# Adding the down projection's results on GpSimd in the next stage, and spreading VectorE's small work

## The chip, the cores and the metric

One core of a Trainium2 chip runs the whole kernel. The metric is the device time of one execution in microseconds, and lower is better. Profile figures come from one profiled execution.

## The reference

2048 rows (tokens) of 1024 columns pass through three residual blocks: a gated feed-forward with 4-bit weights, a state-space convolution along the 1024 columns, and the same feed-forward again.

```python
def _dequant(qweight, scales, qzeros, g_idx):
    # W[k,n] = scales[g_idx[k],n] * (w4[k,n] - (z4[g_idx[k],n]+1)), groups of 128 rows
def _L0_ffn_ref(x, ...):                     # 1024 -> 2752 -> 1024
    h = jax.nn.silu(xf @ Wg) * (xf @ Wu)
    out = h @ Wd
def _L0_attn_ref(u, ...):                    # one S4 response K for all rows
    y = irfft(rfft(u, n=2*L) * rfft(K, n=2*L), n=2*L)[..., :L]
    return y + D[0] * u
x = L0_attn_u                                # (2, 1024, 1024)
x = x + 0.5 * _L0_ffn_ref(_layernorm(x), ...)
x = x + _L0_attn_ref(_layernorm(x), ...)
x = x + 0.5 * _L0_ffn_ref(_layernorm(x), ...)   # the same weights
```

## The kernel before, in words

**Jobs.** The rows are cut into four blocks `b` of 512 rows, each of four tiles of 128 rows. A block goes through the feed-forward twice (k = 1 and k = 3), so there are eight jobs (b, k) in the order (0,1), (1,1), (0,3), (1,3), (2,1), (3,1), (2,3), (3,3). Each job has two stages. *Up* (`gate_up`) has 64 steps: eight waves of weight columns times eight groups of 128 input rows. A wave has three pairs of gate and up columns (six units of 128 columns; waves 5 and 6 have two pairs, the last two and a half). *Down* (`down`) has 44 steps: two halves `a` of 512 output columns times 22 tiles of the inner 2752.

**Scaling in the bank.** Each group of 128 input rows has its own scale, so after a group's products a PSUM bank is multiplied by the ratio of this group's scale to the next one's, and the next group's products are added to it. This is `scaled`: on ScalarE (L729) for units with an even number, else on VectorE (L733); some odd units go to ScalarE too, in jobs and steps listed in `gate_up`. TensorE multiplies each weight tile by two parts of the input, `xTh` (float32r) and `xTl` (float16), L764; in down by `hh` and `hl`, L840. At a wave's end ScalarE takes silu (L792), VectorE multiplies gate and up (L795), and GpSimd splits the result in two (L797, L799).

**Weights.** They are kept in DRAM as signed bytes. SP loads the bytes of a step four steps ahead (`b`, `bd`; L690, L697), and GpSimd casts them three steps ahead (L706; in job 0 ScalarE casts some). Job 0 also makes those bytes from the packed words on the way (`raw`, L580 to L584 on VectorE).

**Results of down.** They come out transposed. ScalarE and VectorE write them, scaled, into `yT[a]`; VectorE transposes it in blocks of 32 (`turn_block`, L875); SP writes it to DRAM (`rows_out`, `yz`) and reads it back by rows (`rows_in`, `yr`); VectorE adds it to x in pieces of 256 columns (`back`, L893). Half 0 of a job goes through this in the second half of the same down, half 1 in the first steps of the next job's up. Only the last half of the last job goes through TensorE instead: 16 transposes into PSUM (`back_by_products`, L899) and four adds of 512 columns (L901).

**Normalization.** `moments_by_tile` takes two statistics a tile of rows (L189) and joins them (L192); `guess` starts an inverse square root from the bits (L199 to L203), and `deviations` refines it by three of Newton's steps of three small operations each (L214 to L216) and one last multiply (L217), all on 128 x 4 elements. After k = 1, the next job's up also holds the convolution of the block that has just come out of its first feed-forward: norm (L225), transposes, products (L1197), adds (L1227 to L1237), then moments and `deviations` again for k = 3. `normalize` (L258) is the norm of the next job's input. Job 1's up also makes the response tables (`s4_tables`, between L927 and L1170) in pieces.

**Order.** `hooks` hold work by step: `at(up, s, f)` calls f at step s of up, `at(dn, d, f)` at step d of down; half steps lie in the middle of a step's products. `in_order_of_writing(f, engine)` keeps the instructions of f behind what was written before for that engine. What is not pinned so is placed by a list scheduler with its own estimates, and TensorE, VectorE, ScalarE, GpSimd and SP each run their list strictly in order.

Of the kernel before, what the change touches and what calls it, by code (L numbers as in the profile page):

```python
# [18 lines left out]
ALU = mybir.AluOpType  # L19
# [38 lines left out]
def macaron_s4_kernel(  # L58
# [149 lines left out]
    def deviations(b, k, factor=1.0):  # L208


        mv, ve, r = ln.pop(b)
        e = small.tile([P, NT], F32, tag="e", name=f"e_{b}_{k}")
        for three in (3.0, 12.0, 768.0):
            nc.vector.tensor_tensor(e, r, r, ALU.mult)  # L214
            nc.vector.tensor_tensor(e, e, ve, ALU.mult)
            nc.vector.scalar_tensor_tensor(r, e, three, r, ALU.subtract, ALU.mult)  # L216
        nc.vector.tensor_scalar(r, r, -factor / 8192, None, ALU.mult)  # L217
        for t in range(NT):
            ln[b, t] = (mv[:, t, 0:1], r[:, t : t + 1], k)
        return r  # L220
# [198 lines left out]
    def scales_down():  # L419
        ps = bank("ps_d")  # L420
        for i in range(2):
            row, turn = t2(f"drow_{i}"), t2(f"dturn_{i}")
            nc.sync.dma_start(row[:GD], down_s[:, bass.ts(i, 512)])
            nc.vector.tensor_copy(by_chunk(turn[:GD]), by_block(row[:GD]))
            for k in range(4):
                nc.tensor.transpose(
                    ps[:, bass.ts(4 * i + k, GD)], turn[:GD, bass.ts(k, P)], ident[:GD, :GD]
                )
        n = NC * GD
        flat = s_dn.rearrange("p c g -> p (c g)")  # L430
        nc.vector.tensor_copy(flat, ps[:, :n])
        inv = t2("inv_d")[:, :n]
        inverse(inv, flat, "d")
        inv = inv.rearrange("p (c g) -> p c g", c=NC)
        nc.vector.tensor_tensor(
            ratd[:, :, : GD - 1], s_dn[:, :, : GD - 1], inv[:, :, 1:], ALU.mult
        )
        nc.vector.tensor_scalar(
            ratd[:, :, GD - 1 :], s_dn[:, :, GD - 1 :], 0.5 / EIGHT, None, ALU.mult
        )  # L440
# [294 lines left out]
    def gate_up(j, b, hooks):  # L735
        hi, lo = pieces[b]
        ps = {}
        for s, (wi, g) in enumerate(STEPS):
# [13 lines left out]
            for i, (k, pos, done) in enumerate(turns):  # L752
# [21 lines left out]
                if g < GK - 1:  # L774
                    on_act = unit % 2 == 0
                    if pos == 1:
                        on_act = (j == 0 and g % 4 == 0) or (j == 1 and s < 32 and g % 2 == 0)
                        on_act = on_act or (j in (2, 5, 6) and 10 <= s < 20 and g % 2 == 0)
# [84 lines left out]
    by_products = lambda j, a: j == len(JOBS) - 1 and a == NH - 1  # L863
# [24 lines left out]
    def back(b, a, i):  # L888

        t, half = divmod(i, 2)  # L890
# [573 lines left out]
    def rows_home(at, hooks, b, a, turned_at, out_at, in_at, added_at):  # L1464

        pinned = lambda f, *e: lambda: in_order_of_writing(f, *e)
        for i in range(8):
            at(hooks, turned_at[i], pinned(lambda i=i: turn_block(a, i), ET.DVE))
            at(hooks, added_at[i], pinned(lambda i=i: back(b, a, i), ET.DVE))
        for i in range(4):  # L1470
            at(hooks, out_at[i], pinned(lambda i=i: rows_out(a, i), ET.SP))
            at(hooks, in_at[i], pinned(lambda i=i: rows_in(b, a, i), ET.SP))

    def fast():
# [5 lines left out]
        for j, (b, k) in enumerate(JOBS):  # L1480
# [7 lines left out]
            pinned = lambda f, *e: lambda: in_order_of_writing(f, *e)  # L1488
            if prev:
                pb, pk = prev  # L1490
                turned_at = [i / 2 for i in range(8)]
                added_at = [10 + (i if j == 1 else i / 2) for i in range(8)]
                rows_home(at, up, pb, 1, turned_at, (5, 5, 6, 6), (8, 8, 9, 9), added_at)
                if pk == 1:
                    late = 34 if j == 1 else 14
                    first = 30 if j == 1 else 14
                    steps = [(up, first + (5 * i // 4 if j == 1 else (3 * i // 2) / 2)) for i in range(8)]
                    in_pieces(at, steps, lambda: moments_by_tile(pb, 2, halves=True))
                    at(up, late + 7, pinned(lambda: deviations(pb, 2), ET.DVE))
# [19 lines left out]
                    at(up, late + 27, lambda: moments(pb, 3))  # L1519
                    at(up, late + 28, lambda: deviations(pb, 3, LIFT))  # L1520
# [5 lines left out]
                    at(up, late + 28, save)  # L1526
# [9 lines left out]
            if j == 0:  # L1536
# [6 lines left out]
                at(up, 40, scales_down)  # L1543
# [13 lines left out]
            if after:  # L1557
                ab, ak = after
                if ak == 1:
                    at(up, 55 if j == 0 else 6, lambda: load_x(ab, rows_of(u, ab)))  # L1560
                    if j == 0:
                        steps = [(dn, d) for d in range(4, 22, 2)]
                        in_pieces(at, steps, lambda: moments_by_tile(ab, 1, halves=True))
                        newton = lambda: deviations(ab, 1, LIFT)
                        at(dn, 21, lambda: in_order_of_writing(newton, ET.DVE))
                    else:
                        steps = [(up, s) for s in range(18, 27)]
                        in_pieces(at, steps, lambda: moments_by_tile(ab, 1, halves=True))
                        newton = lambda: deviations(ab, 1, LIFT)
                        at(up, 28, lambda: in_order_of_writing(newton, ET.DVE))  # L1570
# [9 lines left out]
                for t in range(NT):  # L1580
                    for half in range(2):
                        d, where = ((22 + 4 * t + 2 * half, dn), (3 * t + half, dn))[min(j, 1)]
                        if j > 1:
                            d, where = (45 if ak == 3 else 31) + 2 * t + half, up
# [3 lines left out]
                    if j == 0:  # L1588
                        for half in range(2):
                            piece = lambda t=t, half=half: turn_by_pool(ab, t, half)  # L1590
                            at(dn, 24 + 4 * t + 2 * half, piece)
# [10 lines left out]
            turned_at = [22.5 + i if j == 0 else 22 + i / 2 for i in range(8)]  # L1602
            added_at = [37.5 + (3 * i // 2) / 2 if j == 0 else 34.5 + i for i in range(8)]
            out_at, in_at = (((31, 31, 32, 32), (35, 35, 36, 36)), ((27, 27, 28, 28), (31, 31, 32, 32)))[min(j, 1)]
            rows_home(at, dn, b, 0, turned_at, out_at, in_at, added_at)
            for t in range(NT) if not after else ():
                at(dn, int(added_at[2 * t + 1]) + 2, lambda t=t: store_half(t, 0, nc.sync))
# [207 lines left out]
```

## Time and profile before

| what | us |
|---|---|
| runs, median of 3 | 2099.97 (2099.79 to 2103.26) |
| the profiled execution | 2098.86 |
| its span, first to last instruction | 2097.1 |
| TensorE busy | 2044.3 |
| VectorE busy | 1722.2 |
| ScalarE busy | 1405.3 |
| GpSimd busy | 1301.5 |

The profiled execution is 1.76 us longer than its span: that lies before the first and after the last instruction. A matmul's record covers its passage through the array and overlaps the next one's, so busy shares of TensorE are no measure of its rate. In the rows, a line such as L733 is the line of the kernel's source, `out<-in` are tiles without numbers, and after the bar stand the busy time of the group in us, the mean of one in ns, and the idle time of its engine just before, with what ended it.

### The profile page before, as it was taken

To read this page: it belongs to the slowest core of one execution; us is meant where nothing else is said; L and a number is where in the kernel's file an instruction comes from. 1 tells how busy PE (TensorE), PEld (TensorE's weight loads), DVE (VectorE), ACT (ScalarE), POOL (GpSimd) and SP (SyncE) were. 2 spreads that over 40 slices of the span, in tenths; PEclk is the share of its full clock that TensorE was granted. 3 is DMA by queue.
4 is the path that set the end of the run, shared out by engine and by line. 5 is a ranking of instruction groups with operands and counts; after the bars stand their busy time and mean duration, and the time that the engine had idled before them with its cause. 6 is when DMAs were issued, how large, how long until landed. Compare 5 with 4: busy or idle time off the path is not lost.

```text
span 2097.1 us, 30092 instructions
## 1 busy us (share of the span) xinstructions
PE 2044.3 (97%) x9316; PEld 1378.3 (66%) x9316; DVE 1722.2 (82%) x2916; ACT 1405.3 (67%) x2200; POOL 1301.5 (62%) x1688
## 2 busy tenths in 40 slices
PE   6999999999999999999999999999999999999998
PEld 4555675577767667655766567676686676866576
DVE  8888978778889878897788878888788878787777
ACT  6777787646675577677767776755777647767775
POOL 5867758646855468555866568544685546865542
PEclk9999999999999999999999999999999999999999
DMA  4324342112621126511462126211163111651113
GB/s 146 117 85 146 111 125 74 34 53 55 167 78 44 42 51 167 158 34 35 113 169 96 31 51 165 81 38 49 38 161 98 40 47 34 161 166 51 35 34 100
DMA packets 280039, 182.47 MB, mean 87 GB/s; under 512 B 100667, under 2 KB 259236, under 8 KB 279870
## 3 DMA queue, kind: packets, MB, share of 16 engines
q1 hardware_dynamic: 278566, 178.06, 30.8%
q8 instruction: 76, 1.25, 0.2%
q10 hardware_dynamic: 1016, 1.82, 0.2%
q14 instruction: 93, 0.76, 0.1%
q0 software_dynamic: 288, 0.59, 0.1%
HBM read 120.18 MB, written 41.23 MB: 77 GB/s over the span
## 4 chain that ended last, share of the span: by engine, by line
PE 86%; DVE 7%; DMA 2%; POOL 2%; issue 1%; ACT 1%; SPq 0%; ACTq 0%; POOLq 0%; DVEq 0%
PE pg L764 52%; PE po L840 28%; PE pc L1197 3%; DVE pg L733 2%; PE pb L1197 1%; DMA bd<-wdq 1%; DVE po L733 1%; PE st L232 1%; DVE x L893 1%; DMA b<-wq 1%; POOL q L613 0%; POOL hl L799 0%; DVE x L258 0%; DVE ve L199 0%; DMA x<-in_L_attn_u_dram 0%
## 5 line engine op out<-in xcount | busy, mean ns | idle before, releaser
L729 ACT ACTIVATE pg<-pg,rat 128x512 f32<-128x512 f32 x1255 | 794.5, 661 | 388.0 <-PE pg L764 387.0
L733 DVE TENSOR_TENSOR pg<-pg,rat 128x512 f32<-128x512 f32 x1153 | 765.4, 693 | 140.8 <-PE pg L764 130.8
L764 PE MATMUL pg<-xTh,w_up 128*128 128x512 f32 x2752 | 856.3, 439 | 7.3 <-DVE pg L733 4.4
L764 PE MATMUL pg<-xTl,w_up 128*128 128x512 f16 x2752 | 718.4, 382 | 11.3 <-DVE pg L733 4.9
L706 POOL CAST w_up<-b 128x768 fp32r<-128x768 int8 (+2 forms) x490 | 381.8, 786 | 498.6 <-PE pg L764 400.1
L764 PEld LDWEIGHTS pg<-xTh,w_up 128*128 128x128 f32 x2752 | 520.1, 189 | 189.8 <-DVE pg L733 22.5
L729 ACT ACTIVATE po<-po,ratd 128x512 f32<-128x512 f32 x660 | 431.4, 661 | 159.4 <-PE po L840 158.7
L840 PE MATMUL po<-hl,w_down 128*128 128x512 f32 x1344 | 529.7, 400 | 5.7 <-DVE po L733 5.3
L840 PE MATMUL po<-hh,w_down 128*128 128x512 f32 x1344 | 517.2, 391 | 0.0
L733 DVE TENSOR_TENSOR po<-po,ratd 128x512 f32<-128x512 f32 x620 | 425.9, 694 | 91.0 <-PE po L840 88.2
L764 PEld LDWEIGHTS <-w_up 128*128 128x128 bf16 x2752 | 227.0, 99 | 336.7 <-issue 157.4
L706 POOL CAST w_down<-bd 128x512 fp32r<-128x512 int8 x352 | 220.1, 631 | 157.1 <-PE po L840 75.9
L840 PEld LDWEIGHTS po<-hl,w_down 128*128 128x128 f32 x1344 | 250.2, 188 | 94.4 <-DVE po L733 29.3
L840 PEld LDWEIGHTS po<-hh,w_down 128*128 128x128 f32 x1344 | 252.5, 188 | 47.7
L799 POOL TENSOR_TENSOR hl<-hf,hh 128x512 fp32r<-128x512 f32 x168 | 219.2, 1305 | 7.2
L792 ACT ACTIVATE g<-pg,rat 128x512 f32<-128x512 f32 x168 | 111.1, 687 | 74.2 <-PE pg L764 63.1
L795 DVE SCALAR_TENSOR_TENSOR hf<-pg,rat,g 128x512 f32<-128x512 f32 x168 | 122.6, 747 | 45.1 <-ACT g L792 36.4
L797 POOL CAST hh<-hf 128x512 fp32r<-128x512 f32 x168 | 108.7, 647 | 53.9 <-DVE hf L795 28.3
L893 DVE TENSOR_TENSOR x<-x,yr 128x256 f32<-128x256 f32 x120 | 73.1, 615 | 3.0 <-DMA yr<-yz 3.0
L284 POOL TENSOR_TENSOR lo<-x,hi 128x512 f16<-128x512 f32 x48 | 62.2, 1296 | 0.0
L189 DVE BATCH_NORM_STATS2 stats<-x 128x6 f32<-128x512 f32 x88 | 60.0, 685 | 0.6
L298 POOL TENSOR_TENSOR xTh<-turned 128x512 fp32r<-128x512 bf16 x48 | 56.5, 1177 | 0.0
(219 smaller groups left out, 1110.1 us busy)
## 6 DMA issues: line engine op xcount, KB each, us to landing
b<-wq SPq DMA_DIRECT2D x319, 96.0 KB
bd<-wdq SPq DMA_DIRECT2D x336, 64.0 KB
x<-in_L_attn_u_dram SPq DMA_DIRECT2D x30, 512.0 KB
yz<-y SPq DMA_DIRECT2D x60, 256.0 KB
yr<-yz SPq DMA_DIRECT2D x60, 256.0 KB
b<-wq SPq DMA_DIRECT2D x128, 64.0 KB
xs<-x SPq DMA_DIRECT2D x16, 512.0 KB
x<-xs SPq DMA_DIRECT2D x16, 512.0 KB
```

What stands on the lines that cost most here:

```text
L284: nc.gpsimd.tensor_tensor(lo[:, own], n[:, own], hi[:, own].bitcast(F32), ALU.subtract)
L706: nc.gpsimd.tensor_copy(t, b)
L729: nc.scalar.activation(dst, src, AF.Copy, scale=sc)
L733: nc.vector.tensor_tensor(dst, src, sc.to_broadcast(list(dst.shape)), ALU.mult)
L764: nc.tensor.matmul(p, weights, (lo, hi)[k][:, g, :], start=(g == 0 and not done), stop=(g == GK - 1 and done), skip_group_check=True,)
L792: nc.scalar.activation(g, pg, AF.Silu, scale=rat[:, 2 * f, GK - 1 :])
L795: nc.vector.scalar_tensor_tensor(hf, pu, last, g, ALU.mult, ALU.mult)
L797: nc.gpsimd.tensor_copy(hi, hf)
L799: nc.gpsimd.tensor_tensor(lo, hf, hi.bitcast(F32), ALU.subtract)
L840: nc.tensor.matmul(ps[c], w[:, bass.ts(c, P)], part, start=(f == 0 and k == 0), stop=(f == NF - 1), skip_group_check=True,)
L893: nc.vector.tensor_tensor(part, part, rows_back[a, t][:, own], ALU.add)
L1197: nc.tensor.matmul(dst, lhsT, rhs, start=start, stop=stop, skip_group_check=True)
```

## The change

- `back` becomes one GpSimd add of 512 columns for each tile of rows, instead of two VectorE adds of 256. Half 0's reload and adds move from the down to steps 0 to 3 and 3 to 6 of the next job's up; half 1's adds move from step 10 on to steps 11 to 14. The last job's half 0 keeps VectorE's adds (`back_by_vector`).
- Half 0 of job 0 goes by products (`back_by_products`), at steps 32, 35, 38 and 41 of its down.
- VectorE's block transposes of half 0 are spread over steps 22 to 27 of a down instead of 22 to 25.5.
- `deviations` becomes a generator: each of Newton's three steps and the last multiply is placed in a step (or half step) of its own. The moments for k = 3 after the convolution come in pieces too.
- The odd units of jobs 2, 5 and 6 in steps 10 to 19 stay on VectorE.
- The scales of down are loaded in the order of columns that they are used in, by eight DMAs instead of two, and the two copies that reordered them (L424) go.
- Some steps of normalization move by one to five.

```diff
-        return r
+        ln[b, 0, "r"] = r
...
+    def deviations_in_pieces(b, k, factor=1.0):
...
             nc.vector.scalar_tensor_tensor(r, e, three, r, ALU.subtract, ALU.mult)
+            yield
         nc.vector.tensor_scalar(r, r, -factor / 8192, None, ALU.mult)
...
-    def scales_down():
+    def scale_rows_down():
+        got = [t2(f"drow_{i}") for i in range(2)]
+        for i, row in enumerate(got):
+            src = by_block(down_s[:, bass.ts(i, 512)])
+            for c in range(4):
+                nc.sync.dma_start(row[:GD, bass.ts(c, P)].rearrange("p (a i) -> p a i", i=Q), src[:, :, c])
+        return got
+
+    def scales_down(rows):
         ps = bank("ps_d")
-        for i in range(2):
-            row, turn = t2(f"drow_{i}"), t2(f"dturn_{i}")
-            nc.sync.dma_start(row[:GD], down_s[:, bass.ts(i, 512)])
-            nc.vector.tensor_copy(by_chunk(turn[:GD]), by_block(row[:GD]))
+        for i, row in enumerate(rows):
...
                         on_act = (j == 0 and g % 4 == 0) or (j == 1 and s < 32 and g % 2 == 0)
-                        on_act = on_act or (j in (2, 5, 6) and 10 <= s < 20 and g % 2 == 0)
...
-    by_products = lambda j, a: j == len(JOBS) - 1 and a == NH - 1
+    by_products = lambda j, a: (j, a) in ((0, 0), (len(JOBS) - 1, NH - 1))
...
-    def back(b, a, i):
-
-        t, half = divmod(i, 2)
+    def back(b, a, t):
+
+        part = x[b][t][:, bass.ts(a, 512)]
+        nc.gpsimd.tensor_tensor(part, part, rows_back.pop((a, t)), ALU.add)
+
+    def back_by_vector(b, a, t, half):
+
         own = bass.ts(half, 256)
...
-                turned_at = [i / 2 for i in range(8)]
-                added_at = [10 + (i if j == 1 else i / 2) for i in range(8)]
-                rows_home(at, up, pb, 1, turned_at, (5, 5, 6, 6), (8, 8, 9, 9), added_at)
+                if not by_products(j - 1, 0):
+                    results_in(at, up, pb, 0, (0, 1, 2, 3))
+                    for t in range(NT):
+                        at(up, 3 + t, pinned(lambda t=t: back(pb, 0, t), ET.Pool))
+                results_out(at, up, 1, [i / 2 for i in range(8)], (5, 5, 6, 6))
+                results_in(at, up, pb, 1, (8, 8, 9, 9))
+                for t in range(NT):
+                    at(up, 11 + t, pinned(lambda t=t: back(pb, 1, t), ET.Pool))
                 if pk == 1:
-                    late = 34 if j == 1 else 14
-                    first = 30 if j == 1 else 14
+                    late, first = (33, 27) if j == 1 else (16, 15)
...
-                    at(up, late + 7, pinned(lambda: deviations(pb, 2), ET.DVE))
+                    steps = [(up, late + 4 + i) for i in range(4)]
+                    in_pieces(at, steps, lambda: deviations_in_pieces(pb, 2))
...
-                    at(up, late + 27, lambda: moments(pb, 3))
-                    at(up, late + 28, lambda: deviations(pb, 3, LIFT))
+                    steps = [(up, late + 15 + 4 * t + i) for t in range(NT) for i in range(2)]
+                    in_pieces(at, steps, lambda: moments_by_tile(pb, 3, halves=True))
+                    steps = [(up, late + 29 + i / (2 if j == 1 else 1)) for i in range(4)]
+                    in_pieces(at, steps, lambda: deviations_in_pieces(pb, 3, LIFT))
...
-                at(up, 40, scales_down)
+                at(up, 36, lambda: rows.update(down=scale_rows_down()))
+                at(up, 40, lambda: scales_down(rows.pop("down")))
...
-                        newton = lambda: deviations(ab, 1, LIFT)
-                        at(dn, 21, lambda: in_order_of_writing(newton, ET.DVE))
+                        steps = [(dn, d) for d in (20.5, 21, 21.5, 22)]
+                        in_pieces(at, steps, lambda: deviations_in_pieces(ab, 1, LIFT))
...
-                        newton = lambda: deviations(ab, 1, LIFT)
-                        at(up, 28, lambda: in_order_of_writing(newton, ET.DVE))
+                        steps = [(up, s) for s in range(28, 32)]
+                        in_pieces(at, steps, lambda: deviations_in_pieces(ab, 1, LIFT))
...
-                        d, where = ((22 + 4 * t + 2 * half, dn), (3 * t + half, dn))[min(j, 1)]
+                        d, where = ((23 + 4 * t + 2 * half, dn), (3 * t + half, dn))[min(j, 1)]
                         if j > 1:
-                            d, where = (45 if ak == 3 else 31) + 2 * t + half, up
+                            d, where = (50 if ak == 3 else 33) + 2 * t + half, up
...
-            turned_at = [22.5 + i if j == 0 else 22 + i / 2 for i in range(8)]
-            added_at = [37.5 + (3 * i // 2) / 2 if j == 0 else 34.5 + i for i in range(8)]
-            out_at, in_at = (((31, 31, 32, 32), (35, 35, 36, 36)), ((27, 27, 28, 28), (31, 31, 32, 32)))[min(j, 1)]
-            rows_home(at, dn, b, 0, turned_at, out_at, in_at, added_at)
...
+            if by_products(j, 0):
+                for t in range(NT):
+                    at(dn, 32 + 3 * t, lambda t=t: back_by_products(b, 0, t))
+            else:
+                turned_at = [22 + (3 * i // 2) / 2 for i in range(8)]
+                results_out(at, dn, 0, turned_at, (29, 29, 30, 30))
+            if not after:
+                results_in(at, dn, b, 0, (33, 33, 34, 34))
...
+                        at(dn, 36 + 1.5 * t + 0.5 * half, pinned(piece, ET.DVE))
```

## The prediction

> **What bounds the kernel now.** I read the engine table first, then the chain, the waits, and the timeline around the places that the change touches. From the page (engine table; chain by engine; the row of the adds):
>
> ```profile
> PE 2044.3 (97%) x9316; PEld 1378.3 (66%) x9316; DVE 1722.2 (82%) x2916; ACT 1405.3 (67%) x2200; POOL 1301.5 (62%) x1688
> PE 86%; DVE 7%; DMA 2%; POOL 2%; issue 1%; ACT 1%; SPq 0%; ACTq 0%; POOLq 0%; DVEq 0%
> L893 DVE TENSOR_TENSOR x<-x,yr 128x256 f32<-128x256 f32 x120 | 73.1, 615 | 3.0 <-DMA yr<-yz 3.0
> ```
>
> TensorE bounds it; 97% busy, but a matmul's record overlaps its neighbour's, so I measured loss by starts instead. Unhindered matmuls in the timeline start 0.227 us apart (float32, 512 columns), 0.216 (float16), 0.111 (128 columns) or 0.216 (256 columns). Counting each stage's matmuls at these spacings and taking that from the stage's length gives what is lost: e.g. job 1's down, 344 x 0.227 = 78.1 of 81.9 us. Lost: job 0 up 21 and down 10, job 1 up 17 and down 4, later ups 3 to 7 each, later downs 2 to 3 each; 97 us in all. Only this can be won. Who owns it is in the waits of the weight loads:
>
> ```profile
> PEld po L840 <- DVE po L733: 29.3, 82, 1.8
> PEld pg L764 <- DVE pg L733: 22.5, 54, 1.9
> ```
>
> L733 is VectorE scaling a bank that the next group's matmul adds to. A bank is needed again 8 to 9 matmuls (1.9 us) after it was finished, the scaling and its signal take 0.9, so VectorE may be about 1 us late; more stops TensorE. It is late where other work stands ahead in its queue. Adds first, the timeline of job 4's down:
>
> ```profile
> 1302.18 1.17 POOL L282 TENSOR_TENSOR mid<-hi,top 128x512 bf16<-128x512 f32 x1
> 1302.30 1.33 DVE L893 TENSOR_TENSOR x<-x,yr 128x256 f32<-128x256 f32 x1
> ...
> 1303.55 1.28 DVE L733 TENSOR_TENSOR po<-po,ratd 128x512 f32<-128x512 f32 x2
> 1303.57 0.39 PE L840 MATMUL po<-hh,w_down 128*128 128x512 f32 x1
> ...
> 1304.29 0.50 PE L840 MATMUL po<-hl,w_down 128*128 128x512 f32 x1 [0.33 <-DVE po L733]
> ```
>
> The add waits for GpSimd's L282 to end (1.33 us where its fastest takes 0.41), the scalings start late, and two matmuls start 0.72 apart instead of 0.23: 0.5 us lost. Newton's steps do the same; timeline of job 1's up, VectorE and then GpSimd:
>
> ```profile
> 415.06 1.21 DVE L214 TENSOR_TENSOR e<-r 128x4 f32<-128x4 f32 x1
> 416.98 1.20 DVE L216 SCALAR_TENSOR_TENSOR r<-e,r 128x4 f32<-128x4 f32 x1
> 419.31 1.21 DVE L215 TENSOR_TENSOR e<-e,ve 128x4 f32<-128x4 f32 x1
> ```
> ```profile
> 414.97 1.28 POOL L799 TENSOR_TENSOR hl<-hf,hh 128x512 fp32r<-128x512 f32 x1
> 416.88 1.27 POOL L799 TENSOR_TENSOR hl<-hf,hh 128x512 fp32r<-128x512 f32 x1
> 419.22 1.28 POOL L799 TENSOR_TENSOR hl<-hf,hh 128x512 fp32r<-128x512 f32 x1
> ```
>
> Four-column operations of 0.16 us median take 1.2, each ending with a GpSimd operation.
>
> **What the Trainium skill says.** "SBUF — State Buffer", Who interferes with whom: a VectorE instruction with two SBUF inputs contends with a GpSimd instruction that reads SBUF, and whichever comes second blocks fully. The trace agrees (1.33 against 0.41; 1.21 against 0.16). One SBUF input and one from PSUM does not contend: L901, 0.68 us in all four records. "GPSIMD Engine Reference", Engine selection: two-input elementwise work is about twice slower on GpSimd. The trace: 1.28 us for 512 columns (L799) against twice L893's median 0.428.
>
> **The change part by part.** "Lost" below is start-to-start loss whose last other VectorE work was the named line.
>
> 1. *Adds to GpSimd.* 15 halves x 8 = 120 VectorE adds. 13 halves become 4 adds of 512 columns on GpSimd: 52, nearest row L799, 1.28 us, 67 us of GpSimd; 104 x 0.615 = 64 us leave VectorE. Job 7's half keeps its 8. In downs 1 to 6 L893 cost 0.86, 0.73, 0.89, 1.33, 0.46, 1.32 = 5.6 us; the slots become empty and nothing replaces them, so I take 5.0 (3 to 6; the spread transposes L875 remain, 0.2 a stage). In job 1's up the add waited 3.0 us for its DMA with scalings behind it, 1.6 lost, and more beside L984: 2.0 (1 to 2.5). In ups 2 to 7 the adds cost nothing visible. Price on GpSimd: an add stands in its queue between weight casts (L706, 0.83 median), which is what TensorE waits for behind it. A wide step is 6 x (0.227 + 0.216) = 2.66 us; cast plus add is 2.1, and casts run three steps ahead, so ups 2 to 7 cost 0. In job 1 the response tables keep GpSimd busy (busy by window: all of 318 to 329 us, 1.9 of the 6 us to 335, 11.4 of the 12 us to 347): of 5.1 us of adds 4.1 fit, so casts and tables slip by about 1 us, and adds collide with L984: -0.8 (0 to -4). The reloads of the first half (4 DMAs of 256 KB on SP) go from the down to the next up's steps 0 to 3, between loads `b`; they were written 14 steps earlier. By window that stretch moves 45 to 54 GB/s in jobs 2, 5, 6 and 165 in jobs 3, 4, 7 (x of the next job, now behind them; its first use is step 18), against 181 where they leave the down. Cost 0 while the loads' lead of four steps holds. SP's stores at steps 13 to 16 now wait for GpSimd's adds of steps 11 to 14, two steps earlier: 0, down to -1 a job for jobs 3, 4 and 7 if GpSimd lags.
>
> 2. *Newton and moments in pieces.* Ten dependent operations become four groups in four steps. Lost in ups: job 1 about 5.0, job 2 2.5, jobs 5 and 6 1.5 each = 10.5; jobs 3 and 4 none. A wide step leaves VectorE 2.66 - 3 x 0.60 = 0.86 us (0.60 is one scaling after another); three small operations need 0.3 to 0.5, or 1.5 when one meets an L799. So a piece mostly fits, but the built order still puts the last ones between the L795s at a wave's end, where L799 runs. I take half, 5.5 (0 to 9).
>
> 3. *ScalarE's help withdrawn.* Jobs 2, 5, 6, steps 10 to 19: 15 scalings go from ScalarE (0.66) to VectorE (0.60). Adds are gone from there. In steps 15 to 20, moments need 8 x 0.60 + 4 x 0.12 = 5.3 us of 6 x 0.86 = 5.2: full, inside the 1 us of slack: -0.8 (0 to -3).
>
> 4. *down_s.* The two copies L424 go; TensorE lost 1.26 + 0.22 on them. Eight DMAs of 84 pieces of 128 bytes take their place, ahead of `raw_7` on SP, 0.33 to 0.4 us an issue: about 3 us of SP near 130 us, and loads `b_0_43` on come 5 us later than 133. They are cast near 147. TensorE meets ps_d at step 40 (146.5), over 10 us after the issue. +1.4 (-1 to 1.7).
>
> 5. *Job 0's first half by products.* 16 TensorE transposes at 0.11 = -1.75, four L901-like adds (0.68), in place of 8 L875 (0.43), 8 L893 and 8 DMAs. x was loaded from 224 to 245 us, before its first use near 267. Of the 10 us lost there, L875 owns 1.7 and L893 0.5, some 1.5 of which goes; L258 (up to 2.42 us behind GpSimd) stays. -0.3 (-2.5 to +1.5).
>
> Sum: 5.0 + 2.0 - 0.8 + 5.5 - 0.8 + 1.4 - 0.3 = 12.0 us. The span is 2097.1, the profiled execution 2098.86, so 2086.9 for it; that execution lies 1.1 under the median of the runs, 2099.97, so the median becomes 2088.0.
>
> **Rivals.**
> - *Adds help, pieces don't.* Each of Newton's operations still meets a GpSimd operation, only in four places. For it: the built order at wave ends. Against: jobs 3 and 4 lose nothing even in one piece. Without the 5.5: 2093.5.
> - *Costs eat it.* Moments without ScalarE overrun (-3 each in three jobs) and job 0 loses 2.5: about 2098. For it: VectorE at 98% in those steps. Against: no stop of TensorE there now.
> - *GpSimd becomes the bound (slower).* In steps 3 to 6 and 11 to 14 the add blocks the queue while its reload is late; casts slip, TensorE waits. It decides when an add is late by more than the casts' lead, some 5 to 8 us (2 to 3 steps). The DMA of job 1 was 3 us late already. 13 groups x 1.3 us beyond the lead = 17, plus gains lost: 2098.86 + 17 - 10 + 1.1, about 2107. Against: GpSimd spends 400 us waiting for TensorE in L706, so it leads almost everywhere.
>
> **How the numbers follow.** 0.2% is 4.2 us, about what a measurement of this kernel can tell from no change: 2095.8 to 2104.2 counts as the same. Forecast 0.55 (2083 to 2093), adds only 0.23, costs eat it 0.13, GpSimd bound 0.09. Faster: 0.55 + 0.21 + 0.02 = 0.78; same 0.02 + 0.11 = 0.13; slower 0.09. The parts' good ends together reach -22 (2078); leaving the slower case and half of the even one out gives 2099 as upper end.
>
> **What would show it.** Right: L893 falls to 8 instructions, GpSimd shows 52 adds near 1.3 us; waits of po on L733 drop from 29 to near 20 us; downs 2 to 6 lose about 1.5 us each; L214 to L216 near 415 us no longer stand in one row of 1.2 us. Step 5 is right if job 0's down keeps its 92 us within 2. Wrong: waits of TensorE on L706 above 10 us, L189 ahead of stops in jobs 2, 5, 6 (steps 15 to 20), or job 1's up longer than 201 us.

## The result, and the profile after

| | before | after |
|---|---|---|
| runs of both on one chip, median (us) | 2101.61 (2099.79 to 2103.67) | 2078.53 (2076.89 to 2081.12) |
| profiled execution (us) | 2098.86 | 2081.12 |
| its span (us) | 2097.1 | 2079.2 |

The ratio of the times is 0.9891, 95% interval 0.9874 to 0.9908: some 23 us faster, 19 to 27 by the interval. The forecast was 12 us. The profiled execution of before is the fastest of its runs and that of after the slowest, so the two spans show only 17.9 us; another profile of after, taken with the first experiments, has a span of 2077.6 (19.5 us). Runs of one kernel lie some 4 us apart here, so the spans and the medians don't contradict each other.

From the page of after: engine table, chain by engine, the row of the new adds, and then two lines of its waits (waiting line, what released it: us in total, times, longest).

```profile
PE 2031.7 (98%) x9332; PEld 1388.2 (67%) x9332; DVE 1670.2 (80%) x2813; ACT 1398.8 (67%) x2185; POOL 1352.6 (65%) x1740
PE 89%; DVE 6%; POOL 2%; DMA 1%; issue 1%; ACT 1%; SPq 0%; ACTq 0%; POOLq 0%; DVEq 0%
L900 POOL TENSOR_TENSOR x<-x,yr 128x512 f32<-128x512 f32 x52 | 66.7, 1284 | 0.0
```
```profile
PEld po L849 <- DVE po L743: 15.6, 32, 2.3
PEld pg L774 <- DVE pg L743: 12.3, 41, 1.0
```

The work has moved as the diff says: 52 adds of 1.28 us on GpSimd, 67 us in all, and VectorE 52 us less busy. L743 is the scaling on VectorE that was L733 (L774 and L849 are the matmuls L764 and L840). TensorE's waits on it fell from 29.3 to 15.6 us in the downs and from 22.5 to 12.3 in the ups. That is where the gain is. The stages, measured from first matmul to first matmul in the trace (us; "downs 2-6" and "ups 2, 5, 6" are sums; the last row is for the part on the clock below):

| stage | before | after | after, again | adds undone | transposes undone | Newton undone | Newton alone | two waits moved |
|---|---|---|---|---|---|---|---|---|
| job 0 up | 177.3 | 181.6 | 180.4 | 179.6 | 178.9 | 181.1 | 178.3 | 176.6 |
| job 0 down | 92.0 | 91.2 | 91.3 | 92.9 | 91.2 | 91.1 | 92.0 | 91.3 |
| job 1 up | 200.8 | 193.0 | 193.0 | 195.1 | 191.6 | 196.0 | 194.8 | 193.3 |
| job 1 down | 81.9 | 84.7 | 84.7 | 85.1 | 85.4 | 85.0 | 87.7 | 83.6 |
| ups 2, 5, 6 | 562.7 | 555.6 | 555.7 | 555.1 | 555.6 | 564.8 | 554.7 | 554.9 |
| downs 2-6 | 402.3 | 393.4 | 393.4 | 397.6 | 395.9 | 393.1 | 401.6 | 393.1 |
| the rest | 579.9 | 579.8 | 579.1 | 579.7 | 579.3 | 579.2 | 580.2 | 579.2 |
| in them, TensorE at half clock, before the tail | 10.2 | 17.1 | 10.2 | 13.7 | 3.4 | 23.9 | 6.8 | 6.8 |

After against before: job 1's up -7.8, downs 2 to 6 -8.9, ups 2, 5 and 6 -7.2; against that, job 0's up +4.3 (+3.1 in the second profile) and job 1's down +2.7. The last two were not forecast.

**What the prediction left out: a stop in job 1's down, and the clock of TensorE.** Job 1's down of after, answer by windows (busy us and matmuls by engine; PEclk is the clock that TensorE was granted, 1.00 is full), then VectorE's and GpSimd's timeline there:

```profile
492.00:494.00 2.00, 0.47 (x1) 0.19 (x1) 1.94 (x3) 0.50 (x1) 1.86 (x3) 1.00 0.02 2
495.00:498.00 3.00, 3.00 (x9) 2.31 (x8) 2.69 (x4) 0.84 (x2) 2.50 (x4) 0.57 0.09 25
498.00:500.00 2.00, 2.00 (x10) 1.43 (x9) 1.72 (x3) 1.14 (x2) 1.42 (x3) 1.00 0.11 33
```
```profile
492.37 1.33 DVE L263 TENSOR_SCALAR x<-x,mv,r 128x512 f32<-128x512 f32 x1
493.74 1.30 DVE L743 TENSOR_TENSOR po<-po,ratd 128x512 f32<-128x512 f32 x2
494.94 1.54 DVE L263 TENSOR_SCALAR x<-x,mv,r 128x512 f32<-128x512 f32 x1
```
```profile
492.16 1.27 POOL L808 TENSOR_TENSOR hl<-hf,hh 128x512 fp32r<-128x512 f32 x1
...
494.93 1.27 POOL L825 TENSOR_TENSOR hb<-hf_half,hb 64x512 fp32r<-64x512 f32 x1
```

The normalization L263 (0.53 us at its fastest) ends 0.3 us after GpSimd's split L808, the scaling L743 stands behind it, and TensorE stops for 2.2 us. Then nine matmuls start in 3 us where at full clock ten start in 2. In this trace the clock fell to half in four places before the tail, for 3.4 us or twice that each. The Trainium skill, "TensorE: Matmul & The Clock Gate", Part 1: The HAM clock gate, describes two clocks, half and full, and a free-running window of 3413 ns. The lengths of 3.4 us agree. It puts the fall after an idle window of about 3.4 us; here a stop of 2.2 us among sparse matmuls came before the fall, and the measurement decides.

A stretch of 3.4 us does 1.7 us of work, so it costs at most 1.7 us (an estimate from its length). Here it cost less. The runs with the old scales, with the bare blocks and without products share this stage with after and have the same stop of 2.2 us, but no half-clock stretch behind it: job 1's down takes 84.3 us in each, and 84.7 in after. So the loss there is the stop, and the clock adds 0.4 us. In job 1's up, after and its second profile have a stretch at 363 to 365 us and take 193.0 us; the runs with the old scales and with the transposes undone share that stage, have no stretch, and take 191.9 and 191.6. There it costs 1.1 to 1.4 us. Why one execution meets a stretch and another does not is open; such differences may be part of the 4 to 6 us between runs of one kernel, which is not shown. Parts below some 3 us are therefore read from stages here, not from medians, and with an eye on the stretches in the stage.

### The profile page after: what moved, and what is told of

Read it like the earlier page. It is cut to its first block, busy times and chain, and to the rows that moved or that the text cites. A ratio compares the mean times of both kernels' runs of the same rounds, so it can differ in the third digit from the quotient of the medians.

```text
span 2079.2 us, 30011 instructions
## 1 busy us (share of the span) xinstructions
PE 2031.7 (98%) x9332; PEld 1388.2 (67%) x9332; DVE 1670.2 (80%) x2813; ACT 1398.8 (67%) x2185; POOL 1352.6 (65%) x1740
## 4 chain that ended last, share of the span: by engine, by line
PE 89%; DVE 6%; POOL 2%; DMA 1%; issue 1%; ACT 1%; SPq 0%; ACTq 0%; POOLq 0%; DVEq 0%
PE pg L774 55%; PE po L849 29%; PE pc L1210 3%; DVE pg L743 1%; PE pb L1210 1%; DMA b<-wq 1%; DVE po L743 1%; PE st L237 1%; DVE x L263 0%; POOL q L623 0%; DMA x<-in_L_attn_u_dram 0%; DVE hf L804 0%; POOL w_up L716 0%; DMA wq<-q 0%; DVE xn L230 0%
## 5 line engine op out<-in xcount | busy, mean ns | idle before, releaser
L743 DVE TENSOR_TENSOR pg<-pg,rat 128x512 f32<-128x512 f32 x1168 | 775.3, 692 | 162.3 <-PE pg L774 154.2
L774 PE MATMUL pg<-xTh,w_up 128*128 128x512 f32 x2752 | 851.4, 437 | 2.4 <-DVE pg L743 1.8
L774 PE MATMUL pg<-xTl,w_up 128*128 128x512 f16 x2752 | 717.6, 383 | 12.8 <-DVE pg L743 6.9
L716 POOL CAST w_up<-b 128x768 fp32r<-128x768 int8 (+2 forms) x490 | 375.4, 772 | 429.6 <-PE pg L774 323.0
L774 PEld LDWEIGHTS pg<-xTh,w_up 128*128 128x128 f32 x2752 | 520.6, 189 | 178.7 <-issue 14.3
L849 PE MATMUL po<-hl,w_down 128*128 128x512 f32 x1344 | 528.8, 396 | 6.1 <-DVE po L743 5.3
L849 PE MATMUL po<-hh,w_down 128*128 128x512 f32 x1344 | 520.9, 391 | 0.0
L743 DVE TENSOR_TENSOR po<-po,ratd 128x512 f32<-128x512 f32 x620 | 429.1, 695 | 110.5 <-PE po L849 108.7
L774 PEld LDWEIGHTS <-w_up 128*128 128x128 bf16 x2752 | 226.6, 99 | 338.5 <-issue 159.5
L716 POOL CAST w_down<-bd 128x512 fp32r<-128x512 int8 x352 | 217.1, 620 | 149.7 <-PE po L849 87.8
L849 PEld LDWEIGHTS po<-hl,w_down 128*128 128x128 f32 x1344 | 251.7, 188 | 76.9 <-DVE po L743 15.6
L849 PEld LDWEIGHTS po<-hh,w_down 128*128 128x128 f32 x1344 | 253.0, 188 | 50.2
L808 POOL TENSOR_TENSOR hl<-hf,hh 128x512 fp32r<-128x512 f32 x168 | 219.4, 1306 | 8.0
L804 DVE SCALAR_TENSOR_TENSOR hf<-pg,rat,g 128x512 f32<-128x512 f32 x168 | 123.5, 747 | 42.3 <-ACT g L801 33.3
L900 POOL TENSOR_TENSOR x<-x,yr 128x512 f32<-128x512 f32 x52 | 66.7, 1284 | 0.0
L287 POOL TENSOR_TENSOR mid<-hi,top 128x512 bf16<-128x512 f32 x48 | 56.0, 1167 | 0.0
```

What stands on the lines that cost most here:

```text
L716: nc.gpsimd.tensor_copy(t, b)
L743: nc.vector.tensor_tensor(dst, src, sc.to_broadcast(list(dst.shape)), ALU.mult)
L774: nc.tensor.matmul(p, weights, (lo, hi)[k][:, g, :], start=(g == 0 and not done), stop=(g == GK - 1 and done), skip_group_check=True,)
L804: nc.vector.scalar_tensor_tensor(hf, pu, last, g, ALU.mult, ALU.mult)
L808: nc.gpsimd.tensor_tensor(lo, hf, hi.bitcast(F32), ALU.subtract)
L849: nc.tensor.matmul(ps[c], w[:, bass.ts(c, P)], part, start=(f == 0 and k == 0), stop=(f == NF - 1), skip_group_check=True,)
```

## The experiments

Ratios are to the kernel before, run beside each kernel (2099.6 to 2100.2 us). Each kernel is the changed kernel with one edit, except where its part says otherwise.

**The changed kernel again.** 

> The changed kernel once more, as the common measure of this group and to see which stage lengths repeat. In its first profile, job 0's up took 181.6 us (177.3 before) with a 2.3 us stop at L384 near 156 us, and TensorE's clock was granted at half in four stretches (6.8 + 3.4 + 3.4 + 3.4 us) before the tail. Theory A (the stop belongs to the order of VectorE's and GpSimd's work): 181 to 182 again, and about 22 us under the kernel before. Theory B (chance of that one execution): job 0's up back at 177 to 179. Downs 2 to 6 at 78.6 to 78.9 under both.

2080.33 us, ratio 0.9905 (0.9890 to 0.9921). It is the base for the others. Its downs repeat, and job 0's up keeps 3.1 of its 4.3 us.

**Adds undone.**

```diff
-                    for t in range(NT):
-                        at(up, 3 + t, pinned(lambda t=t: back(pb, 0, t), ET.Pool))
...
+                    for i in range(8):
+                        piece = lambda i=i: back_by_vector(b, 0, i // 2, i % 2)
+                        at(dn, 34.5 + i, pinned(piece, ET.DVE))
```
(half 0 in the same down again, on VectorE; half 1 likewise on VectorE, from step 10 of the up)

> The changed kernel with all adds on VectorE again, in halves, at the old steps (half 0 in the same down, half 1 from step 10 of the next up); job 0's first half stays by products, Newton stays in pieces. Theory A (the adds own the gain in the downs and part of job 1's up): downs 2 to 6 back from 78.6 to about 80.5 us each, job 1's up 2 to 3 us longer, ups 2, 5, 6 about 1 longer each: 14 us more than the changed kernel. Rival B (only the losses that I had put on L893, 5.6 us over six downs, belong to them): 7 to 8 us more. Rival C (VectorE had room): within 2 us.

2085.54 us, ratio 0.9926 (0.9912 to 0.9940): 5 us, less than either of the first two expectations. Downs 2 to 6 are 4.2 us longer in all, job 1's up 2.0. But these downs stand at 79.5 to 79.7 us, not at the 79.9 to 80.9 of before: half of what the downs won belongs to something else.

**Adds later, but on VectorE.**

```diff
-                        at(up, 3 + t, pinned(lambda t=t: back(pb, 0, t), ET.Pool))
+                        for half in range(2):
+                            piece = lambda t=t, half=half: back_by_vector(pb, 0, t, half)
+                            at(up, 3 + t + half / 2, pinned(piece, ET.DVE))
```
(half 1 likewise, at steps 11 to 14)

> The changed kernel, with the adds where the change put them in the next up, but as VectorE halves in place of GpSimd. If the gain of the adds is of their place (the end of a down is where VectorE has no slack), downs stay at 78.6 and the ups stay within 0.5 us of the changed kernel: run within 1.5 us of it. If it is of the engine, every up from 1 to 7 gets 0.5 to 2 us longer (eight more VectorE instructions for the first half and eight for the second), and the run 4 to 8 us longer. Job 1's up, with its many VectorE pieces, should show it first, 2 us or more.

2080.49 us, ratio 0.9909 (0.9895 to 0.9922). The downs stay at 78.6, and no up from job 2 on is longer by more than 0.1 us. The adds take 0.44 us each on VectorE:

```profile
L906 DVE TENSOR_TENSOR x<-x,yr 128x256 f32<-128x256 f32 x112 | 48.7, 436 | 0.4 <-DMA yr<-yz 0.4
```

So the gain of the downs is of the place, the first steps of an up, not of the engine.

Job 1's up is another matter. It seems only 0.6 us longer (193.6), but the base has a half-clock stretch in it and this profile has none; the two runs without one have 191.6 and 191.9, so the adds cost about 2 us there. TensorE's waits on VectorE from 325 to 345 us, where half 1's adds stand, first here, then with the adds undone (the base has no such wait in this window):

```profile
PEld pg L774 <- DVE pg L743: 2.9, 5, 1.2
```
```profile
PEld pg L774 <- DVE pg L743: 2.2, 2, 1.9
```

In this up, which is full of VectorE's small work, the later steps on VectorE won nothing against the old place; GpSimd's adds did.

**Block transposes undone.**

```diff
-                turned_at = [22 + (3 * i // 2) / 2 for i in range(8)]
-                results_out(at, dn, 0, turned_at, (29, 29, 30, 30))
+                turned_at = [22 + i / 2 for i in range(8)]
+                results_out(at, dn, 0, turned_at, (27, 27, 28, 28))
```


> The changed kernel with one part undone: in the downs, the eight block transposes of the first half's results stand half a step apart again (22 to 25.5) and the transfers out go at 27 and 28. If the spread of these transposes is what the adds' experiment left unexplained (downs of 79.5 us there against 80.5 before), downs 1 to 6 become about 1 us longer each (79.3 to 79.8 in place of 78.6) and the run 4 to 6 us longer than the changed kernel. If, as the prediction had it, the spread is worth 0.2 us a stage at most, downs stay within 0.3 us of 78.6 and the run within 1 us; then the transposes cost only where the adds stood behind them.

2079.88 us, ratio 0.9910 (0.9897 to 0.9924), not to be told from the base. The stages tell it: every down from 2 to 6 is at 79.2 us, 2.5 us in all, and job 1's down 0.7 longer, which is between the two expectations; job 0's and job 1's ups were 1.4 to 1.5 us shorter than in the base, which has two half-clock stretches there that this profile has not. The same line of waits, first with the adds undone, then with the transposes undone (after has 15.6 us, 32 times):

```profile
PEld po L849 <- DVE po L743: 21.1, 46, 2.3
```
```profile
PEld po L849 <- DVE po L743: 17.6, 41, 2.3
```

**Newton in one piece again.**

```diff
-                    steps = [(up, late + 4 + i) for i in range(4)]
-                    in_pieces(at, steps, lambda: deviations_in_pieces(pb, 2))
+                    at(up, late + 7, pinned(lambda: deviations(pb, 2), ET.DVE))
```
(the other three places of `deviations` likewise, the moments stay in pieces)

> The changed kernel with each `deviations` in one piece at one step again, adds on GpSimd. Theory A (pieces are worth what the prediction took, about half of 10.5 us in ups 1, 2, 5, 6): 5 to 6 us more than the changed kernel, 3 of it in job 1's up. Rival B (the losses at Newton's steps came from the adds' backlog and from the place in the wave, not from its length): within 1.5 us. Rival C (one piece also brings back the half-clock stretch of 6.8 us near 419 us): 8 to 10 us more, most of it in job 1's up.

2091.41 us, ratio 0.9959 (0.9946 to 0.9973): 11 us, more than any of the three expectations. Ups 2, 5 and 6 are 9.1 us longer, job 1's up 3.0. Job 6's up at a wave's end: VectorE's timeline, TensorE's first matmul after the stop, and the window behind it:

```profile
1646.66 1.22 DVE L222 TENSOR_SCALAR r<-r 128x4 f32<-128x4 f32 x1
1647.92 1.03 DVE L230 TENSOR_SCALAR xn<-x,mv,r 128x1024 f32<-128x1024 f32 x1
1648.87 1.28 DVE L743 TENSOR_TENSOR pg<-pg,rat 128x512 f32<-128x512 f32 x2
```
```profile
1649.62 0.93 PE L774 MATMUL pg<-xTh,w_up 128*128 128x512 f32 x2 [1.71 <-DVE pg L743]
```
```profile
1650.00:1653.00 3.00, 3.00 (x11) 1.74 (x10) 2.10 (x5) 0.66 (x1) 1.46 (x3) 0.50 0.12 33
```

The last multiplication (L222, four columns) takes 1.22 us beside GpSimd's split, L230 follows it, TensorE waits, and then its clock is at half: 11 matmuls in 3 us. Jobs 2 and 5 have one such stretch each too, at most 1.7 us of their 2.6 and 2.9.

For these three ups the edit does not bring back the kernel before. The changed kernel has other steps, so the first of the two Newton blocks now stands at step 23, the end of a wave; before had it in one piece at step 21, in the middle. TensorE's waits on VectorE's scalings around it in job 6's up, in before (1639 to 1655 us) and here (1635 to 1651 us), and then around the second block here (step 45, 1728 to 1738 us):

```profile
PEld pg L764 <- DVE pg L733: 0.8, 2, 0.5
```
```profile
PEld pg L774 <- DVE pg L743: 2.4, 2, 2.1
```
```profile
PEld pg L774 <- DVE pg L743: 0.2, 1, 0.2
```

The second block, also in one piece, costs next to nothing, and so does the one in ups 3 and 4 (step 28, the middle of a wave): they keep 156.0 us. So the 9.1 us are the price of one piece at a wave's end, and not a loss that before had. In job 1's up before has the block at nearly the same busy place (step 41, here 40), and there the 3.0 us stand for the pieces together with their earlier start (steps 37 to 40).

**Bare blocks on VectorE.**

```diff
+            for s in (44, 52):
+                n = {3: 1, 4: 2, 7: 3}.get(j, 0)     # instructions back to back
+                ... nc.vector.tensor_scalar(x[b][i], x[b][i], 1.0, None, ALU.mult)
```


> The changed kernel with idle work added to three quiet ups, that measures by itself what a closed block on VectorE costs TensorE: one, two and three back-to-back instructions of 128x1024 (a multiplication of dead data by 1, some 1.1 us each) at steps 44 and 52 of job 3's, job 4's and job 7's up. The prediction took half of a Newton block's time as lost. By that, the ups get 1.1, 2.2 and 3.3 us longer (two blocks each). The rival: a slack of some 0.6 us is absorbed and all beyond it is lost, which gives 1, 3.2 and 5.4 us, and where a stop gets near 2 us the TensorE clock falls to half for 3.4 us, another 1.7 us each, so that the longest ups reach 5.4 to 9 us.

2080.57 us, ratio 0.9906 (0.9892 to 0.9921).

```profile
L1640 DVE TENSOR_SCALAR x<-x 128x1024 f32<-128x1024 f32 x12 | 7.7, 683 | 0.0
```

An instruction takes 0.68 us, not 1.1. Two blocks of 0.68, 1.37 and 2.05 us made the three ups 0.1, 0.5 and 1.1 us longer. Both expectations are wrong: by half the blocks' own time it would be 0.7, 1.4 and 2.1; by a slack of 0.6 us it would be more than that for the longest. In the middle of a wave VectorE's lead takes up about 1.5 us (2.05 less the 0.55 lost). So the length of Newton's block is not what made it dear in the run above. It stood at a wave's end, where VectorE has silu's products (L804) to do and GpSimd's splits stop it. The blocks here met no split, and they stand in waves of two pairs; a block at a wave's end was not tried by itself.

**Newton's pieces alone, in the kernel before.** (the same lines of the diff, with the moments and the steps of normalization that go with them, put into the kernel before)

> The kernel before with one part of the change alone: Newton's steps and the moments in pieces, at the steps of the changed kernel; adds, block transposes, job 0's first half and down's scales as before. Undoing this part in the changed kernel cost 11 us. If the parts are independent, it gains 9 to 12 us here, in job 1's up (3 to 8) and in jobs 2, 5 and 6's ups (2 to 3.5 each), and the downs keep their 80 to 81 us. If the pieces gain only where the adds have left VectorE free, which the prediction's 5.5 us would agree with, it gains 4 to 7 us and job 1's up stays above 197.

2090.89 us, ratio 0.9957 (0.9945 to 0.9969): 9.3 us, within the first expectation. Ups 2, 5 and 6 win 8.0 and job 1's up 6.0 (before has a half-clock stretch of 6.8 us there, this profile none); job 1's down loses 5.7, with a stop of 2.2 us and a half-clock stretch in the same place as after. So this part brings its own loss into job 1's down, and its gain does not depend on the adds.

Before loses its time in ups 2, 5 and 6 some 138 to 148 us into each. There the last moments, the guess (L199 to L203) and the second Newton block follow a wave's end. VectorE's timeline in job 6's up:

```profile
1724.05 0.94 DVE L199 TENSOR_SCALAR ve<-mv 128x4 f32<-128x4 f32 x1
...
1725.69 1.20 DVE L203 TENSOR_SCALAR r<-half 128x4 int32<-128x4 int32 x1
```

This block in one piece at step 45 cost nothing in the run above. So the 8.0 us come from the moments in pieces or from the later steps rather than from Newton's pieces; no run separates the two.

**No products in job 0.**

```diff
-    by_products = lambda j, a: (j, a) in ((0, 0), (len(JOBS) - 1, NH - 1))
+    by_products = lambda j, a: (j, a) in ((len(JOBS) - 1, NH - 1),)
```


> The changed kernel, with job 0's first half taken back through the transfers (block transposes, out, in, adds by GpSimd in the next up) and without the 16 transposes on TensorE. The prediction put the products at a net gain of 0.3 us: run within 1 us of the changed kernel, with job 0's down near 90 us (1.75 us of TensorE work less, a little more waiting) and job 1's up longer by 1 to 2 us for the four more adds that its GpSimd gets. The other case: the block transposes collide with the pieces of the next job's normalization in job 0's down, which then stays at 92 us or more, and the products are worth 2 us or more.

2079.65 us, ratio 0.9901 (0.9886 to 0.9916). Job 0's down has the same 91.3 us without the 1.75 us of transposes (the first case had 90, the second 92 or more), but job 1's up is 3.6 us longer. There the matmul of the response tables came before its data:

```profile
400.30 1.13 PE L1164 MATMUL s_t<-s_rows,s_turn 128*128 128x512 f32 x2 [2.60 <-DMA s_rows<-k_dram]
```

A half-clock stretch follows it at 401.5 us. In the base this wait is 0.2 us. Whether the extra transfers or only a different moment made the reload late is not settled, so the products' worth is 0 to 3.6 us.

**ScalarE's help back** (the deleted line restored). 

> The changed kernel with ScalarE's help put back: in steps 10 to 19 of jobs 2, 5 and 6's ups, ScalarE again takes every second of VectorE's scalings at the second place. The prediction gave its withdrawal a price of 0.8 us for the three ups. By that, these ups become 0.2 to 0.3 us shorter each. The other case, that the help had only served the adds and the moments that stood there, leaves them within 0.2 us, or makes them longer where ScalarE is late; either way the run stays within 1.5 us of the changed kernel.

2078.93 us, ratio 0.9899 (0.9886 to 0.9912). Ups 2, 5 and 6 are 1.1 us shorter in all, 0.8 of it in job 2's; the other two are within 0.3, and job 5's up varies by 0.8 among kernels that share it. So withdrawing the help cost about 1 us, mostly in one up.

**Down's scales as before** (two DMAs and two copies again). 

> The changed kernel with down's scales loaded and reordered as before (two DMAs, the two copies L424), all else changed. Theory A: the eight DMAs moved the inverse of the scales (L383, L384) under GpSimd's splits at the end of wave 4[...]; with the copies back, job 0's up returns to about 177.5 us, 4 us less in all. Rival B: the copies cost 1.5 us again as in the prediction, and the rest of the 4.3 us was chance: 1 to 2 us more than the changed kernel.

2078.77 us, ratio 0.9900 (0.9883 to 0.9916). Job 0's up falls from 180.4 to 178.3 us: the new way of loading is dearer, not cheaper. (The nine profiles with the new loads at these steps have 178.6 to 181.6 us, the three with the old ones 177.3 to 178.3.) After's timeline shows it on VectorE, then TensorE:

```profile
153.92 1.39 DVE L383 SCALAR_TENSOR_TENSOR inv_d<-sq_d,s_dn 128x168 f32<-128x168 f32 x1
155.23 0.69 DVE L743 TENSOR_TENSOR pg<-pg,rat 128x512 f32<-128x512 f32 x1
155.83 1.19 DVE L384 RECIPROCAL inv_d<-inv_d 128x168 f32<-128x168 f32 x1
```
```profile
155.97 0.38 PE L774 MATMUL pg<-xTl,w_up 128*128 128x512 f16 x1 [2.14 <-DVE pg L743]
```

Without the copies ahead of it the inversion of the scales comes some 7 us sooner, among GpSimd's splits at the end of a wave (L808 at 153.74 for 1.39 us), and stops TensorE. With the old loads L383 stands at 160.6 us and takes 0.32 us; there TensorE waits 1.1 us for the copies instead.

**The two new waits moved.**

```diff
-                at(up, 40, lambda: scales_down(rows.pop("down")))
+                at(up, 43, lambda: scales_down(rows.pop("down")))
...
-                        d, where = ((23 + 4 * t + 2 * half, dn), (3 * t + half, dn))[min(j, 1)]
+                        d, where = ((23 + 4 * t + 2 * half, dn), (3 * t + half + 2, dn))[min(j, 1)]
...
-                        at(dn, 2 + 9 * t + d, piece)
+                        at(dn, 2 + 9 * t + d + (1 if j == 1 and t == 0 else 0), piece)
```


> The changed kernel with the two waits moved that it gained against the kernel before: the copies that invert down's scales go three steps later in job 0's up (43 in place of 40), behind the splits that GpSimd makes at the end of a wave, and in job 1's down the eight normalizations start two steps later (2 to 13 in place of 0 to 10), behind the last splits of the up. If those GpSimd splits are what held up VectorE there, job 0's up falls from about 181 to 178.5 us and job 1's down from 84.7 to 82.5, and the run is 3 to 5 us faster than the changed kernel. If they are not the cause, the stop moves along with the copies and stages stay within 0.5 us.

2074.33 us, ratio 0.9878 (0.9863 to 0.9893): faster than both kernels, 5.7 us ahead of the changed one by the two ratios. Job 0's up is 176.6 us, job 1's down 83.6. The lines that answer to those of after, the inversion and then the same part of job 1's down with its clock:

```profile
156.14 0.74 DVE L383 SCALAR_TENSOR_TENSOR inv_d<-sq_d,s_dn 128x168 f32<-128x168 f32 x1
...
490.45 1.10 DVE L263 TENSOR_SCALAR x<-x,mv,r 128x512 f32<-128x512 f32 x1
```
```profile
490.00:494.00 4.00, 3.67 (x16) 2.61 (x15) 3.97 (x7) 2.49 (x4) 3.90 (x6) 1.00 0.17 48
```

The inversion takes 0.74 in place of 1.39 us and the normalization 1.10 in place of 1.33. In job 1's down a stop of 1.5 us behind the last splits remains of 2.2. The clock stays at full there, but so it did in three runs with the normalizations unmoved (84.3 us), so that the full clock is not shown to come from the move; of the stage's 1.0 us, 0.7 is the move's.

**Quarters in job 1** (on top of the two moved waits; each normalization as four instructions of 128x256). 

> The changed kernel with both waits moved, and job 1's normalizations also cut into quarters (128x256 each, half a step apart, from step 2). In the kernel with the two waits moved each half still took 0.9 to 1.6 us beside GpSimd's copies and stopped TensorE five times by 0.5 to 0.75 us. If a stop there is the length of one instruction less a fixed slack, quarters stop it hardly at all: job 1's down falls from 83.6 to 81 us, the run by 2 to 3 us to about 2072. If VectorE is short of time there as a whole, quarters change nothing or make it worse by their fixed cost, and the down stays at 83 to 84.5.

2074.69 us, ratio 0.9883 (0.9869 to 0.9898): no better. Job 1's down rises to 85.3 us. Three of its quarters still took 1.3 to 1.4 us beside GpSimd, against 0.40 at the fastest, so a shorter instruction was not stopped for less.

## Why the prediction was right or wrong

The direction and the reason hold: VectorE was late with its scalings because other work stood ahead, and taking that away released TensorE. 2078.53 us is the good end of the range, and that it still lies in it owes something to luck: gains that were taken too small made up for two losses that were not forecast. By its steps:

1. *Adds.* Right in size: 5.0 taken for downs 1 to 6; undoing them costs 4.2 in downs 2 to 6 and 0.5 in job 1's. Job 1's up: 2.0 less 0.8 taken, 2.0 measured. In the downs it was the place that counted, in job 1's up the engine. The charge of 0.8 on GpSimd did not appear: TensorE's waits on its up casts (L716) are 2.9 and 2.1 us in all in after, 3.5 and 2.2 before. **"the slots become empty ... the spread transposes L875 remain, 0.2 a stage" is a step that failed**: their spread is worth about half a microsecond in each of downs 2 to 6 and 0.7 in job 1's, 3.2 us that the sum lacks. I had looked at what the transposes stop now, not at what they do once the scalings are a little late already.
2. *Newton and moments.* **The term that was mis-sized most.** 10.5 us was read as lost, and half taken. Done alone, the part wins 14.1 us in the ups, pays 5.7 in job 1's down, and gains 9.3 by the runs. "Half" came from the operations that still stood between L795s at a wave's end. Some still stand there in job 2's up, after. But those ahead of the wave's end have scalings between them, and even one that takes 0.75 us stops TensorE by no more than 0.1:

```profile
635.66 0.75 DVE L218 TENSOR_TENSOR e<-r 128x4 f32<-128x4 f32 x1
636.33 0.69 DVE L743 TENSOR_TENSOR pg<-pg,rat 128x512 f32<-128x512 f32 x1
636.93 0.15 DVE L219 TENSOR_TENSOR e<-e,ve 128x4 f32<-128x4 f32 x1
```

   What decided was the step as much as the number of pieces. In jobs 2, 5 and 6 a Newton block in one piece cost little at step 21, nothing at step 45 and about 3 us at step 23. The steps that moved along with the pieces had no term of their own in the sum. In job 1's up the gain is of the pieces and their earlier steps together.
3. *ScalarE.* Right in sum: 0.8 taken, 1.1 measured in the three ups, 0.8 of it in job 2's alone.
4. *down_s.* **Wrong in sign**: +1.4 taken, job 0's up 2.1 us longer than with the old loads. I counted the copies that go and the DMAs that come, not what the later instructions meet when they come sooner. With the inversion three steps later this up is 176.6 and (with quarters) 175.7 us, against 177.3 to 178.3 in the three kernels with the old loads, so a gain of about 1 us was there to be had.
5. *Products.* Job 0's down kept 92 us within 2, as said: 91.2. What they are worth lies in job 1's up and is 0 to 3.6 us; -0.3 was low. The four records of L901 don't show that an add with an input from PSUM is not held up: GpSimd did nothing from 2080 to 2092 us, where they lie. The scalings show it: the 1773 L733 on `pg` and `po` in before take 0.66 to 0.70 us each.

Not in the sum: job 1's down, +2.7 us. There Newton's last multiplication between the last products of the wave now takes 0.68 us (L222) in place of 0.16, and the first two normalizations start 0.2 and 0.0 us after a GpSimd split has begun (before 0.6 and 0.7), so that they take 1.33 and 1.54 us (before 1.01 and 0.88). The stop grew from 1.0 to 2.2 us. Newton's pieces alone bring the same stop; with the normalizations two steps later it is 1.5 us.

Set side by side: adds 4.2 + 2.0, transposes 2.5, Newton and moments 14.1 (from the run in the kernel before; undoing Newton measures another place), ScalarE -1.1, scales -2.1, products 0 to 3.6, job 1's down -2.7: 17 to 20.5 us, where the spans show 18 to 19.5. The rival "adds help, pieces don't" falls with the run of that part alone, "costs eat it" with the 1.1 us of ScalarE and job 0's down of 91.2 us, and "GpSimd becomes the bound" with those waits on L716.

## What to carry to other kernels

What small work costs on a shared engine depends on where it stands: 2 us in the middle of a quiet stretch cost half a microsecond, and a chain of tiny operations in one piece cost next to nothing in the middle of a wave and about 3 us at its end, beside an engine that blocks it. So look first where such a chain stands, and move it, or pieces of it, away from the point where the other engine is busiest. When a part is undone to measure it, see that it goes back to its old step, or another place is measured. When something is removed, list what comes sooner because of it, and look at what it will then stand beside: the loss in job 0's up came that way. Shifts by two or three steps won that loss back in full, and 1.0 of the 2.7 us in job 1's down. And compare stages only between profiles with the same clock in them: a missing half-clock stretch hid more than 1 us here.

## What the runs showed of the hardware that was not expected

- A stop of TensorE of about 2 us can be followed by 3.4 us at half clock (PEclk 0.50, 11 matmuls in 3 us where 15 start at full clock). The same stop of 2.2 us in job 1's down was followed by it in some profiles and not in others. It cost 0.4 us there, and 1.1 to 1.4 in job 1's up, less than the 1.7 us of its length.
- GpSimd's adds and VectorE's in the same steps cost TensorE the same in the ups from job 2 on (VectorE's no more than 0.1 us longer), although they take 1.28 us a tile on one and 2 x 0.44 us on the other; in job 1's up VectorE's cost about 2 us.
- 1.37 us of closed VectorE work in the middle of a wave cost TensorE 0.25 us, 2.05 us cost 0.55.
- A VectorE operation on 128 x 4 elements, 0.16 us by itself, takes 1.22 us beside a GpSimd subtraction of 128 x 512 (L222 beside L808).
